# Position bias made beside the first image's tokens, parameter bounds between its scan output chunks, layer 1's inputs in other PSUM banks and its norms in later chunks

## The chip, the cores and the metric

The kernel runs on one core of a Trainium2 chip. The metric is the device time of one execution in microseconds (us); the time of a kernel is the median of its runs. The engines are named as in the profile: PE (TensorE, the matmuls), PEld (its weight loads), DVE (VectorE), ACT (ScalarE), POOL (GpSimd) and SP (SyncE, which only issues DMAs here). Each takes its own instructions in the order that was fixed when the program was built.

## The reference

Four layers, one after the other, on 4 images of 64 x 64 positions with 128 channels, all in float32. Cut to what matters here:

```python
# layer 0: selective scan in four directions k (rows, columns, and both backwards)
xc    = silu(depthwise_conv3x3(ln(x) @ in_proj_x) + conv_b)          # 256 channels
z     = ln(x) @ in_proj_z
delta = softplus(dt_w[k] @ (x_proj[k] @ xc)[:8] + dt_b[k])
h     = exp(delta * A) * h + (delta * xc) * B_t                      # along 4096 positions
y     = sum over k of (h . C_t) + Ds * xc
x     = x + (ln(y) * silu(z)) @ out_proj
x     = x + gelu(ln(x) @ fc1) @ fc2
# layer 1: attention over all 4096 positions, 16 query/key channels
f, g, v = x @ Wq, x @ Wk, x @ Wv
x     = gamma * (v^T softmax(f g^T, over n)) + x
# layer 2: 1x1 and 3x3 convolutions with hard swish
# layer 3: attention in a 7 x 7 neighbourhood, 4 heads, with a position bias rpb, then an MLP
attn  = softmax(q k^T + rpb[relative position]);  x = x + (attn v) @ proj
x     = x + gelu(ln(x) @ fc1) @ fc2
```

The kernel computes the softmaxes of layers 1 and 3 and the softplus of layer 0 without subtracting a maximum. For that it computes bounds of the exponents' sizes from the parameters and from layer 1's queries, keys and values into a tile `K.bounds`. At the end it reads one word made of them, and would do the whole network again in a general form if a bound were exceeded. With these inputs it isn't.

## The kernel before

**Phases.** An image's work has two halves. The first is *scan inputs* (`scan_inputs`): the *tokens* (`scan_tokens`: layer norm, in_proj, 3 x 3 convolution as nine diagonal matmuls L246, SiLU, in 8 chunks of 512 positions) leave `xc` in SBUF; the *steps* (`scan_steps`) make `delta` and `du = delta * xc` (L417 on POOL) and the rows B and C (`bc`) for four directions, and store all of these in DRAM. The scan itself (`selective_scan`) then goes through the directions in the order 1, 3, 0, 2, and in each through 8 chunks, 2 halves, 4 groups of states and 2 pairs: 512 *units* to an image. A unit loads its `bct` on SP, makes `dB` on POOL (L499), two `dA = exp(A * delta)` on ACT (L505, into PSUM), two recurrences on DVE (L507), and two products with C on DVE (L512) or, in 5 of 16 units for the first image and 7 of 16 for the others, one on POOL (L520). PE sums the products (L553). The last direction, 2, goes from chunk 7 to chunk 0 and stores each chunk of `y` in DRAM as it is made.

The second half is `rest`: *scan output* (`scan_output`: in 8 chunks from 7 to 0, load `y`, norm, gate, out_proj and MLP into `xT`; two chunks are under way at a time, each a generator that gives way at its `yield`s; the MLP of layer 3 of the image before runs between them), `layer1`, `layer2`, `layer3_attention`. The last image's `rest` runs after the scan's memory has been given back (`scan_over`), and its attention layers use wider tiles (`wide`).

**Order.** A planner places each instruction when the program is built. Where several are ready for an engine it takes the lowest number. Plain code is numbered from near 0 upwards. `selective_scan` has numbers from 10,000,000 (`SCAN_FIRST`), so the scan fills what the other phases leave. `make_layer2` (folded weights for layer 2, stored in DRAM) has numbers from 5,000,000. Everything of SP goes through one queue in order, ACT's own DMAs through ACT's.

**Memory.** Pools are a stack: a pool opened after another was closed lies in the same bytes, and its tiles wait until the old tiles there are released. In PSUM (8 banks) the scan has 4 (`ss_ps`: three `dA`, one `py`), and the phase beside it the other 4.

**What stands between.** `network` calls, after the first image's scan in the text, `layer0_bound`, `layer3_bound` and `make_bias`, then the scan inputs of images 1 to 3, then `rest` of each image. These first three each open pools of their own, in the 4 PSUM banks and the SBUF that the scan inputs use. `make_bias` makes a table `T` from 256 small matmuls (L1191) and 8 additions (L1194), and from it 12 tiles `bt`: a memset (L1201), three copies out of `T` by DMA (L1212) and one store to DRAM (L1213) each.

**Layer 1's inputs.** `layer1`'s PSUM pool has one buffer for each tag. `ps` is the scores' (2 banks; 4 in the last image), `pa` and `den` have a bank each. `queries` fills `f` by four rounds of two matmuls (L755) and a copy (L756), each round in the same `ps`; `norms` squares on ACT (L744), sums by matmul (L747) and takes the maximum on DVE (L748) into `K.bounds`, again through `ps`; `keys` (L762, L763) and `values` (L770, L771) too. The norms of a block of keys come right after it: for the first one ahead of the values, for three more in chunk 0 of the attention. A step of the attention makes scores (L783), exponentials (L787) and products with `v` (L831).

Of the kernel before, what the change touches and what calls it, by code (L numbers as in the profile page):

```python
# [18 lines left out]

# [404 lines left out]
def make_scan(ctx, tc, K, A):  # L424
# [5 lines left out]
    S.psum = ctx.enter_context(tc.tile_pool(name="ss_ps", bufs=1, space=PSUM))  # L430
# [148 lines left out]
def scan_output(tc, K, A, D, img, xT, last):  # L579

    nc = tc.nc
    with ExitStack() as ctx:
# [68 lines left out]
        before = None if last is None else layer3_mlp(tc, K, A, D, *last, wpool, pool, psum, together)  # L653
# [64 lines left out]
def layer1(tc, K, A, D, img, xT, wide):  # L718
# [6 lines left out]
    with ExitStack() as ctx:  # L725
# [14 lines left out]
        def norms(src, where):  # L740
            if K.general:
                return
            sq = pool.tile([128, 2, LC], F32, name="sq", tag="e", bufs=10 // NP)
            nc.scalar.activation(sq, src, AF.Square)  # L744
            ps = pair()
            for u in range(2):
                nc.tensor.matmul(ps[0:4, u, :], K.quads, sq[:, u, :], start=True, stop=True)  # L747
            nc.vector.tensor_reduce(K.bounds[0:4, img, where : where + 1], ps[0:4, :, :], AX.XY, ALU.max)  # L748

        def queries():  # L750
            for p in range(4):
                quad = span(p, 32)
                ps = pair()
                for u in range(2):
                    nc.tensor.matmul(ps[quad, u, :], Wq, xT[:, span(2 * p + u)], start=True, stop=True)  # L755
                nc.scalar.activation(f[quad], ps[quad], AF.Identity, bias=K.first[quad, :])  # L756
            norms(f, 0)

        def keys(p):
# [4 lines left out]
            norms(g[:, 2 * p : 2 * p + 2, :], 1 + p)  # L764

        def values():
            for p in range(4):
                ps = psum.tile([128, 8, 128], F32, name="ps_v", tag="ps")
                for t in range(8):
                    nc.tensor.matmul(ps[:, t, :], xT[:, span(8 * p + t, 128)], Wv, start=True, stop=True)  # L770
                nc.scalar.activation(v[:, 8 * p : 8 * p + 8, :], ps, AF.Copy, scale=gamma)  # L771
            if not K.general:
                nc.vector.tensor_reduce(
                    K.bounds[:, img, 5:6], v, AX.XY, ALU.max, apply_absolute_value=True
                )

# [45 lines left out]
        for c in range(NCH):  # L822
# [3 lines left out]
            for t in range(8):  # L826
# [26 lines left out]
                if c == 0 and t in (1, 3, 5) and not K.general:  # L853
                    keys((t + 1) // 2)
            finish(c, pa, den)
# [201 lines left out]
def layer0_bound(tc, K, A):  # L1057
# [3 lines left out]
    with tc.tile_pool(name="l0b", bufs=1) as pool, tc.tile_pool(name="l0b_p", bufs=1, space=PSUM) as psum:  # L1061
        load = loader(tc, pool, A, 0)
        w = load("in_proj", [128, DI], A["L0_conv_in_proj_w"][:, :DI])
        ln_w, ln_b = load("ln1_w", [128, 1]), load("ln1_b", [128, 1])
        conv_w, conv_b = load("conv_w", [128, ND, 9]), load("conv_b", [128, ND])
        x_proj, dt_w = load("x_proj_w", [128, ND, 2, 128]), load("dt_w", [128, 2, DI])
        squares = pool.tile([128, DI], F32, name="squares")
        nc.scalar.activation(squares, w, AF.Square, scale=ln_w)
        nc.scalar.activation(w, w, AF.Abs, scale=ln_b)
        for t in (conv_b, x_proj, dt_w):  # L1070
            nc.scalar.activation(t, t, AF.Abs)
        ps = psum.tile([128, 2, ND], F32, name="ps")
        for i, t in enumerate((squares, w)):
            for d in range(ND):
                nc.tensor.matmul(ps[:, i, d : d + 1], t[:, span(d, 128)], K.ones[:, 0:1], start=True, stop=True)
        m = pool.tile([128, ND], F32, name="m")
        nc.vector.tensor_copy(m, ps[:, 0, :])
        nc.gpsimd.tensor_tensor(m, m, bc(K.half, [128, ND]), ALU.pow)
        nc.vector.scalar_tensor_tensor(m, m, C**0.5, ps[:, 1, :], ALU.mult, ALU.add)
        taps = pool.tile([128, ND], F32, name="taps")  # L1080
        nc.vector.tensor_reduce(taps, conv_w, AX.X, ALU.add, apply_absolute_value=True)
        nc.vector.tensor_mul(m, m, taps)
        nc.vector.tensor_add(m, m, conv_b)
        pr = psum.tile([128, 2], F32, name="pr")
        for o in range(2):
            for d in range(ND):
                nc.tensor.matmul(
                    pr[:, o : o + 1], x_proj[:, d, o, :], m[:, d : d + 1], start=(d == 0), stop=(d == ND - 1)
                )
        rows = pool.tile([128, 2], F32, name="rows")  # L1090
        nc.scalar.activation(rows, pr, AF.Identity, bias=K.first2)
        pd = psum.tile([1, 2, 2, DI], F32, name="pd")
        for o in range(2):
            for b in range(2):
                at = slice(64 * b, 64 * b + 1 + R)
                nc.tensor.matmul(pd[:, b, o, :], rows[at, o : o + 1], dt_w[at, o, :], start=True, stop=True)
        most = pool.tile([1, 1], F32, name="most")
        nc.vector.tensor_reduce(most, pd, AX.XYZ, ALU.max)
        nc.vector.tensor_scalar(most, most, STEP_LIMIT, None, ALU.is_le)
        nc.vector.tensor_scalar(K.bounds[0:1, 0, 6:7], most, -1.0, 1.0, ALU.mult, ALU.add)  # L1100


def layer3_bound(tc, K, A):
# [5 lines left out]
    with tc.tile_pool(name="lb", bufs=1) as pool, tc.tile_pool(name="lb_p", bufs=1, space=PSUM) as psum:  # L1109
        load = loader(tc, pool, A, 3)  # L1110
        w = load("qkv_w", [128, 3 * C])
        b = load("bq", [1, 3, C], A["L3_conv_qkv_b"].rearrange("(o p) t -> o t p", o=1))
        ng = load("ng", [1, C], A["L3_conv_norm1_g"].rearrange("p o -> o p"))
        nb = load("nb", [1, C], A["L3_conv_norm1_b"].rearrange("p o -> o p"))
        rp = load("rp", [1, HEADS * 169], A["L3_conv_rpb"].rearrange("(o a) b -> o (a b)", o=1))
        for t in (w, b, ng, nb, rp):
            nc.scalar.activation(t, t, AF.Square)
        ps = psum.tile([1, 3 * C], F32, name="ps")
        nc.tensor.matmul(ps, K.ones[:, 0:1], w, start=True, stop=True)

        r = pool.tile([1, 2 * n + 3], F32, name="r")
        nc.vector.tensor_reduce(r[:, :n], ps.rearrange("o (h d) -> o h d", d=HD), AX.X, ALU.add)
        nc.vector.tensor_reduce(r[:, n : 2 * n], b.rearrange("o t (h d) -> o (t h) d", d=HD), AX.X, ALU.add)
        nc.vector.tensor_reduce(r[:, 2 * n : 2 * n + 1], ng, AX.X, ALU.max)
        nc.vector.tensor_reduce(r[:, 2 * n + 1 : 2 * n + 2], nb, AX.X, ALU.add)
        nc.vector.tensor_reduce(r[:, 2 * n + 2 :], rp, AX.X, ALU.max)
        nc.gpsimd.tensor_tensor(r, r, bc(K.half[0:1, :], [1, 2 * n + 3]), ALU.pow)
        a = pool.tile([1, 1], F32, name="a")
        nc.vector.scalar_tensor_tensor(
# [625 lines left out]
```

## Time and profile before

| | us |
|---|---|
| median of 3 runs | 9234.54 (9232.48 to 9246.47) |
| the profiled execution | 9231.94 |
| its span, first to last instruction | 9230.1 |
| busy: PE, DVE, POOL, ACT | 7385.0, 7119.9, 7049.3, 5664.3 |
| granted TensorE clock, mean | 0.852 |

When the phases run, from the trace (us from the span's start; the scan by its first and last L499, `rest` by its first L596 and the next one's):

| image | tokens | scan | rest |
|---|---|---|---|
| 0 | 18 to 215 | 255 to 2434 | 2338 to 4161 |
| 1 | 608 to 941 | 2434 to 4307 | 4161 to 6125 |
| 2 | 1261 to 1487 | 4307 to 6203 | 6125 to 8079 |
| 3 | 1811 to 2031 | 6203 to 8072 | 8079 to 9230 |

The table gives spans of phases that overlap: while one image is scanned, the scan inputs of all later images (during image 0) or the `rest` of the image before run beside it. A window of the profile gives busy time of each engine within it, with the number of instructions, then the granted TensorE clock, the share of the DMA engines' time and the rate of the transfers. A line of the timeline gives start, duration, engine, line, operation, output and inputs, shapes, how many instructions were merged, and in brackets how long the engine had been idle and what ended that.

### The profile page before, as it was taken

The numbers are of one execution on the slowest core, as the hardware profiler recorded it, in microseconds if no ns is written. First come the engines' busy times: TensorE is split into PE (matmuls) and PEld (weight loads), VectorE is DVE, ScalarE is ACT, GpSimd is POOL, SyncE is SP. The second block draws the span as 40 slices with busy tenths as digits, with TensorE's granted clock in tenths as the row PEclk, the third lists the DMA queues.
The fourth block names the chain that finished last, engine by engine and source line by source line (L and its number), as shares of the span: only waits on it lengthen the run. The fifth ranks groups of instructions, "written<-read, shape, count | busy, mean of one in ns | idle before, by whom it ended". The sixth has DMA issues, their size and how long they took to land. (4 is left out here: it accounts for less than half of the span.)

```text
span 9230.1 us, 99135 instructions
## 1 busy us (share of the span) xinstructions
PE 7385.0 (80%) x30116; PEld 2800.0 (30%) x30116; DVE 7119.9 (77%) x8479; ACT 5664.3 (61%) x11293; POOL 7049.3 (76%) x3064
## 2 busy tenths in 40 slices
PE   7647768697678998887689987877799888877987
PEld 3212222132322232333322232334222323343333
DVE  0698777777899988988899979988899889812433
ACT  4655666666566666666766666667666666554355
POOL 1977988979889988997799979988899889900000
PEclk9658678696789998888889988888899988889989
DMA  2766766767544545555444545565455455520020
GB/s 73 268 219 220 258 216 215 247 211 272 202 150 173 175 159 199 182 205 186 153 171 169 182 166 190 190 207 175 153 187 174 156 195 191 183 68 4 1 83 29
DMA packets 716654, 1581.74 MB, mean 171 GB/s; under 512 B 203317, under 2 KB 328396, under 8 KB 711757
## 3 DMA queue, kind: packets, MB, share of 16 engines
q1 hardware_dynamic: 585805, 1399.10, 44.3%
q10 hardware_dynamic: 130304, 176.19, 5.4%
q8 instruction: 242, 3.96, 0.2%
q14 instruction: 303, 2.48, 0.1%
HBM read 1280.47 MB, written 283.59 MB: 169 GB/s over the span
## 5 line engine op out<-in xcount | busy, mean ns | idle before, releaser
L499 POOL TENSOR_TENSOR dB<-du,bc 128x1024 f32<-128x1024 f32 x2048 | 4791.2, 2362 | 639.1 <-DMA bc<-bc_dram 170.9
L505 ACT ACTIVATE dA<-dt,w_A_log 128x512 f32<-128x512 f32 x4096 | 2777.7, 689 | 553.5 <-DVE hc L507 262.6
L507 DVE TENSOR_TENSOR_SCAN dA<-dA,state,dB 128x512 f32<-128x512 f32 x2128 | 2625.6, 1272 | 339.1 <-POOL dB L499 173.7
L520 POOL TENSOR_TENSOR hc<-hc,bc 128x1024 f32<-128x1024 f32 x832 | 1961.8, 2361 | 165.2 <-ACT state L516 92.3
L507 DVE TENSOR_TENSOR_SCAN hc<-dA,state,dB 128x512 f32<-128x512 f32 x1456 | 1802.9, 1268 | 285.8 <-ACT dA L505 118.1
L512 DVE TENSOR_TENSOR hc<-dA,bc 128x512 f32<-128x512 f32 x2432 | 1561.3, 676 | 121.6 <-PE py L553 112.2
L553 PE MATMUL py<-hc,pick 128*32 128x512 f32 x8192 | 1262.5, 696 | 277.6 <-POOL hc L520 180.0
L514 ACT COPY state<-dA 128x1 f32<-128x1 f32 x2128 | 325.4, 157 | 1295.3 <-DVE hc L512 1270.0
L831 PE MATMUL pa<-e,l_v 128*128 128x512 f32 x2048 | 1069.0, 653 | 10.9 <-ACT e L787 10.7
L783 PE MATMUL pair<-l_g,l_f 32*128 32x512 f32 x2048 | 531.4, 667 | 180.1 <-ACT e L787 134.9
L787 ACT ACTIVATE e<-pair 128x1024 f32<-128x1024 f32 (+1 forms) x448 | 507.8, 1133 | 207.0 <-PE pair L783 205.5
L831 PEld LDWEIGHTS pa<-e,l_v 128*128 128x128 f32 x2048 | 373.5, 199 | 664.3 <-issue 639.3
L553 PEld LDWEIGHTS py<-hc,pick 128*32 128x32 f32 x8192 | 216.9, 118 | 1065.5 <-issue 488.9
L507 DVE TENSOR_TENSOR_SCAN dA<-dA,dB 128x512 f32<-128x512 f32 x304 | 357.3, 1212 | 229.1 <-POOL dB L499 175.7
L409 PE MATMUL ps<-xdbl,w_dt_w 9*128 9x512 f32 x512 | 346.5, 899 | 220.5 <-ACT delta L360 142.4
L1281 PE MATMUL pair<-table,ident 128*128 128x512 f32 x768 | 417.4, 670 | 114.1 <-ACT e L1291 89.7
L246 PE MATMUL ps<-band,w_conv_diag 128*128 128x504 f32 (+3 forms) x1152 | 493.1, 586 | 3.4 <-ACT band L315 1.7
L417 POOL TENSOR_TENSOR du<-delta,xc 128x1024 f32<-128x1024 f32 x128 | 333.8, 2611 | 191.0 <-ACT delta L360 179.6
L200 PE MATMUL ps<-ident,ln_xn 128*128 128x128 f32 x512 | 129.7, 350 | 313.1 <-ACT ln_xn L197 240.9
L1291 ACT ACTIVATE e<-pair 128x1024 f32<-128x1024 f32 (+1 forms) x224 | 254.3, 1135 | 149.4 <-PE pair L1285 149.0
L218 PE MATMUL ps<-xnT,w_fc_w 128*128 128x512 f32 x512 | 281.6, 687 | 71.5 <-ACT xnT L201 29.4
L246 PEld LDWEIGHTS ps<-band,w_conv_diag 128*128 128x128 f32 x1152 | 217.3, 190 | 279.1 <-issue 257.8
(276 smaller groups left out, 8616.2 us busy)
## 6 DMA issues: line engine op xcount, KB each, us to landing
bc<-bc_dram SPq DMA_DIRECT2D x1024, 512.0 KB
dt<-delta_dram SPq DMA_DIRECT2D x512, 512.0 KB
du<-du_dram SPq DMA_DIRECT2D x512, 512.0 KB
delta_dram<-delta ACTq DMA_DIRECT2D x128, 512.0 KB
du_dram<-du SPq DMA_DIRECT2D x128, 512.0 KB
table<-biasT_dram SPq DMA_DIRECT2D x72, 512.0 KB
y_first_dram<-y_sum ACTq DMA_DIRECT2D x128, 256.0 KB
y_before<-y_first_dram SPq DMA_DIRECT2D x128, 256.0 KB
```

What stands on the lines that cost most here:

```text
L246: mm = nc.tensor.matmul(out[:, r0 - row0 : r1 - row0, c0:c1], lhsT((dy + 1) * 3 + dx + 1), src[:, r0 + dy : r1 + dy, c0 + dx : c1 + dx], s ...
L409: nc.tensor.matmul(pd[:, d, :], dt_w[rows, o, d * 128 : (d + 1) * 128], xdbl[rows, i, :], start=True, stop=True,)
L499: nc.gpsimd.tensor_mul(dB, dus[pp], mid(bct[:, 0, :], 2))
L505: nc.scalar.activation(dA, dts[pp][:, g, :], AF.Exp, scale=S.A[:, k, j, pr, g : g + 1])
L507: nc.vector.tensor_tensor_scan(hg[:, order], dA[:, order], dB[:, g, order], 0.0 if i == 0 else state[:, j, pr, g : g + 1], ALU.mult, ALU.add,)
L512: mm = nc.vector.tensor_mul(hc[:, g, :], dA, bct[:, 1, :])
L520: made.append(nc.gpsimd.tensor_mul(hc, hc, mid(bct[:, 1, :], 2)))
L553: mm = nc.tensor.matmul(py[0][32 * q : 32 * q + 32, :], S.pick, hcs[q // 2][:, q % 2, :], start=(k == 1 and j == 0), stop=(j == NJS - 1),)
L783: nc.tensor.matmul(ps[:, u, :], f[quad, t // 4, span(t % 4, 128)], g[quad, c, :], start=True, stop=True)
L787: made = nc.scalar.activation(e, ps, AF.Exp)
L831: nc.tensor.matmul(pa, v[:, 8 * q + t, :], es[q], start=(t == 0 and q == 0), stop=(t == 7 and q == 3),)
L1281: nc.tensor.matmul(ps[:, u, :], K.ident, t[:, u, :], start=True, stop=False)
```

## The change

- `make_bias` moves to the start of the program, ahead of the scan inputs of image 0 in the text, with `make_layer2`'s numbers (from 5,000,000). It and `make_layer2` take SBUF from the other end (`side="right"`), one after the other in the same bytes; the bias's PSUM pool is the 4 banks that the scan will use. `bt` has one buffer instead of two. The scan's PSUM pool is opened later, at that same end.
- `layer0_bound` and `layer3_bound` become generators that use `scan_output`'s pools and give way after each matmul group. In the first image's scan output they run between the chunks, in the place that layer 3's MLP has for later images. `layer0_bound` takes its last maximum in four parts.
- `queries` does all eight matmuls into one `ps` tile, neighbours writing to different quarters of its partitions, and one copy. `values` goes through `pa` and `den` in turn, 8 tiles of one bank instead of 4 of two.
- The norms, and the maximum over `v`, move from behind queries, keys and values to the fourth step of chunks 1 to 5.

```diff
 def network(tc, A, out):
             make_conv_diagonals(tc, K, A, D.conv_diag)
-            with tc.tile_pool(name="mk_w2", bufs=1) as pool:
-                with priority(tc, K, SCAN_FIRST // 2):
+            with priority(tc, K, SCAN_FIRST // 2):
+                make_bias(tc, K, A, D.biasT)
+                with tc.tile_pool(name="mk_w2", bufs=1, side="right") as pool:
                     make_layer2(tc, K, A, D, pool)
-                scan_inputs(tc, K, A, D, 0)
+            scan_inputs(tc, K, A, D, 0)
+            S.psum = scan_ctx.enter_context(tc.tile_pool(name="ss_ps", bufs=1, space=PSUM, side="right"))
...
                 if img == 0:
-                    layer0_bound(tc, K, A)
-                    layer3_bound(tc, K, A)
-                    make_bias(tc, K, A, D.biasT)
                     for later in range(1, B):
                         scan_inputs(tc, K, A, D, later)
 def scan_output(tc, K, A, D, img, xT, last):
-        before = None if last is None else layer3_mlp(tc, K, A, D, *last, wpool, pool, psum, together)
+        before = None
+        if last is not None:
+            before = layer3_mlp(tc, K, A, D, *last, wpool, pool, psum, together)
+        elif not K.general:
+            before = chain(layer0_bound(tc, K, A, wpool, psum), layer3_bound(tc, K, A, wpool, psum))
 def layer1(tc, K, A, D, img, xT, wide):
         def queries():
-            for p in range(4):
-                quad = span(p, 32)
-                ps = pair()
-                for u in range(2):
-                    nc.tensor.matmul(ps[quad, u, :], Wq, xT[:, span(2 * p + u)], start=True, stop=True)
-                nc.scalar.activation(f[quad], ps[quad], AF.Identity, bias=K.first[quad, :])
-            norms(f, 0)
+            ps = pair()
+            for u in range(2):
+                for p in range(4):
+                    nc.tensor.matmul(ps[span(p, 32), u, :], Wq, xT[:, span(2 * p + u)], start=True, stop=True)
+            nc.scalar.activation(f, ps, AF.Identity, bias=K.first)
         def keys(p):
...
             nc.scalar.copy(g[:, 2 * p : 2 * p + 2, :], ps)
-            norms(g[:, 2 * p : 2 * p + 2, :], 1 + p)
         def values():
-            for p in range(4):
-                ps = psum.tile([128, 8, 128], F32, name="ps_v", tag="ps")
-                for t in range(8):
-                    nc.tensor.matmul(ps[:, t, :], xT[:, span(8 * p + t, 128)], Wv, start=True, stop=True)
-                nc.scalar.activation(v[:, 8 * p : 8 * p + 8, :], ps, AF.Copy, scale=gamma)
-            if not K.general:
+            for n in range(8):
+                ps = psum.tile([128, 4, 128], F32, name="ps_v", tag=("pa", "den")[n % 2])
+                for q in range(4):
+                    nc.tensor.matmul(ps[:, q, :], xT[:, span(8 * q + n, 128)], Wv, start=True, stop=True)
+                nc.scalar.activation(v[:, n::8, :], ps, AF.Copy, scale=gamma)
+        def bounds(n):
+            if n == 0:
+                norms(f, 0)
                 nc.vector.tensor_reduce(
                     K.bounds[:, img, 5:6], v, AX.XY, ALU.max, apply_absolute_value=True
                 )
+            else:
+                norms(g[:, 2 * n - 2 : 2 * n, :], n)
...
                 if c == 0 and t in (1, 3, 5) and not K.general:
                     keys((t + 1) // 2)
+                if c > 0 and t == 3 and c <= 5 and not K.general:
+                    bounds(c - 1)
 def make_bias(tc, K, A, out):
-        pool = ctx.enter_context(tc.tile_pool(name="bias", bufs=1))
-        psum = ctx.enter_context(tc.tile_pool(name="bias_p", bufs=4, space=PSUM))
+        pool = ctx.enter_context(tc.tile_pool(name="bias", bufs=1, side="right"))
+        psum = ctx.enter_context(tc.tile_pool(name="bias_p", bufs=4, space=PSUM, side="right"))
...
-                bt = pool.tile([128, HEADS, RC, W], F32, name="bt", bufs=2)
+                bt = pool.tile([128, HEADS, RC, W], F32, name="bt")
```

## The prediction

> **What bounds the kernel now.** I read the busy time by stage first, since the page's shares average over stages with different limits. The cuts are events of the timeline: the scan's products L499 run from 255 us, and those of its four images end at 2434, 4307, 6203 and 8072; the later layers of each image (its first L596) begin at 2338, 4161, 6125 and 8079.
>
> ```profile
> core 0: us, PE busy (x) PEld busy (x) DVE busy (x) ACT busy (x) POOL busy (x), PEclk, DMA share, GB/s
> 520.00:766.00 246.00, 98.88 (x566) 34.30 (x566) 233.15 (x288) 123.58 (x304) 178.62 (x82) 0.58 0.75 238
> 766.00:950.00 184.00, 166.66 (x496) 66.22 (x497) 139.32 (x163) 121.88 (x253) 134.69 (x59) 0.95 0.55 192
> 1260.00:1490.00 230.00, 201.75 (x606) 78.88 (x604) 170.47 (x216) 153.81 (x339) 160.43 (x69) 0.92 0.54 178
> 1770.00:1886.00 116.00, 77.63 (x242) 27.98 (x243) 100.47 (x147) 79.05 (x189) 102.33 (x45) 0.76 0.61 217
> 4161.00:4600.00 439.00, 321.06 (x1300) 159.46 (x1300) 367.90 (x521) 311.98 (x692) 345.52 (x149) 0.84 0.51 172
> 4600.00:5346.00 746.00, 657.62 (x2664) 201.39 (x2664) 683.92 (x727) 484.84 (x919) 726.66 (x315) 0.93 0.50 173
> 8072.00:8385.00 313.00, 240.75 (x892) 137.34 (x890) 55.91 (x204) 161.65 (x338) 2.07 (x1) 0.87 0.17 53
> ...
> ```
>
> POOL is the scan's limit: beside layer 1 (4600 to 5346) it is busy 97%. A unit of the scan (one L499; 512 to an image) costs POOL 2.36 us, plus 2.36 for the share that L520 does there (5 of 16 units in the first image, 7 of 16 later): 3.10 and 3.39 us. That turns POOL time into units. But the scan isn't the only chain. The later layers of images 0, 1 and 2 follow one another without a gap (2338, 4161, 6125, 8079), each taking some 1955 us against the scan's 1870 to 1900, and they fall behind: the second image's begin 146 us before its scan ends, the third's 78 us, the last's 7 us after. So **the chain of later layers sets the end**: the last image's scan output runs alone (8072 to 8385, POOL idle), though seven of its eight inputs were ready.
>
> The second view is the timeline of SyncE and ScalarE around 760 us.
>
> ```profile
> 748.60 1.67 SPq L490 DMA_DIRECT2D bc<-bc_dram  x1
> 750.39 3.79 SPq L1213 DMA_DIRECT2D biasT_dram<-bt  x2
> ...
> 766.61 1.28 ACT L342 ACT_TABLE_LOAD   x1
> 767.90 1.27 ACT L342 ACTIVATE xc<-ps,w_conv_b 128x512 f32<-128x512 f32 x2
> ```
>
> The second image's first xc is written 12 us after the last bias store is issued, although its tokens had begun at 608. xc lies where the bias pool lay, and waits for it. Steps of the first image end near 520; then come the bounds (to 553) and the bias (to 766). The second image's tokens end at 941, the third's take 226 us (1261 to 1487). Without the two they would end near 520 + 226 = 746: **195 us** earlier, and with them all scan inputs and the 2338.
>
> The third view is layer 1's start in the last image.
>
> ```profile
> 8385.05 1.90 PE L755 MATMUL pair<-xT,w_Wq 128*32 128x512 f32 x4 [0.84 <-DVE x L1570]
> 8387.13 1.10 ACT L756 ACTIVATE l_f<-pair,first 32x1024 f32<-32x1024 f32 x1 [3.63 <-PE pair L755]
> 8388.29 1.90 PE L755 MATMUL pair<-xT,w_Wq 128*32 128x512 f32 x4 [1.33 <-ACT l_f L756]
> ...
> 8398.68 3.56 PE L747 MATMUL pair<-sq,quads 128*4 128x512 f32 x4 [2.28 <-ACT sq L744]
> 8402.33 1.21 DVE L748 TENSOR_REDUCE bounds<-pair 4x1 f32<-4x1024 f32 x1 [17.33 <-PE pair L747]
> 8403.60 1.98 PE L762 MATMUL pair<-xT,w_Wk 128*128 128x512 f32 x4 [1.36 <-DVE bounds L748]
> ```
>
> One buffer, `ps`, holds everything, so PE, ScalarE and DVE take turns. From the first query to the first `pa` (8431.47) it takes 46 us.
>
> **The change, part by part.** The sum is made against the profiled execution (9231.9 us, span 9230.1). The median is 2.6 above it.
>
> A. Bias and bounds leave the first scan. From 520 to 766 POOL did 178.6 / 3.10 = 58 units. At the rate with least beside it (1770 to 1886: 102.3 / 3.10 = 33 units, 3.51 us each) these take 202 us, so 44 were lost. Part of that is tokens work that comes anyway: tokens cost the scan 230 - 51.7 x 3.51 = 48 us (1260 to 1490) and only 31 of it shows after 766. 44 - 17 = 27: **-27** (0 to -44). The bounds' small instructions come back beside the first image's scan output, which then waits for the scan; cover gone, they cost their old 33 us (520 to 553), in the high end.
>
> B. Bias beside the first tokens (0 to 255). Its 256 matmuls L1191 take 14.9 us of a PE that is busy 199 of 255; half: **+8**. DVE is busy 14 us of the 255 and hides the 12 memsets (21.2 us). The 36 copies and 12 stores join SyncE's queue, in order, ahead of x loads; `bt` has one buffer now, so a store waiting for its copies holds the loads behind it. Two x buffers cover one chunk, some 25 us, against 163 / 12 = 14 us a group in the busy queue of before. make_layer2 follows the bias in the same bytes, and its L873 (20.8 us on POOL) can land on the scan's start: high end 14.9 + 20.8 = 36. Low end 0.
>
> C. The later layers start earlier. Scan inputs done 195 us sooner, the first image's scan output can follow the scan's last direction (1886 to 2434), chunk by chunk. It then ends with that scan plus one chunk: 65 us (the first chunk took 2342 to 2406). Before, layer 1 began 204 us after the scan's end, when POOL had done 178.4 / 3.39 = 53 units (2434 to 2641); now 17. The lead is 36 units, at layer 1's 3.48 us (746 us for 214 units) **125 us**. What is late next is the scan itself, so 195 isn't kept.
>
> D. Layer 1's inputs. Queries: 16 instructions with neighbours in other column quarters. L553 is of that kind: 8 in 1.06 us (timeline), so 2.1 us and one copy of 1.10 in place of four rounds of 3.1. Keys 1.98 and 1.01. Values: 8 x 1.03 us, in two other banks, while ScalarE copies. First `pa` after some 14 us, not 46: -32. The three norms in chunk 0 held the scores 3.2 us each (8445.6 to 8448.8): -10. Later, each of five costs PE 1.88 and, at worst, reduce 1.3 and an exposed wait on `e` of 2.0; 3.6 taken: +18. So **-24** in the last image (-6 to -33), and -23 in each other one.
>
> The Trainium skill, TensorE: Matmul & The Clock Gate, section Part 3: Packing small matmuls, says that a weight load overlaps matmuls in flight only when its row group differs, which speaks against the queries' new order, as all four share the 128 rows. By it 16 loads at the measured 0.11 us of L755 would be exposed, an estimate of 1.8 us. L553's row, same shape, shows 8 loads and matmuls in 1.06 us, so I leave it out.
>
> E. What the lead is worth. 125 + 3 x 23 = 194 us before the last image. One chunk of scan output beside the scan takes 439 / 8 = 55 us, so 3.5 chunks move under the scan. Alone each takes 306 / 8 = 38. Under it, each costs the scan (439 - 101.8 x 3.48) / 8 = 10.6. Net -27.5 each: **-96** (1 chunk -27, 6.5 chunks -179).
>
> Sum: -27 + 8 - 24 - 96 = -139, so 9093 for the execution and **9095 us** for the median. Its own range, from the terms' ends, is 8980 (-44, 0, -33, -179) to 9210 (0, 36, -6, -27 give 9237, all four at once being rare).
>
> **Rivals.** *The lead goes nowhere* (0.17). POOL's 97% beside layer 1 says that each engine's fixed order ties the later layers to the scan's units; shorter preludes then only leave less room for units. Against it: the lag does grow, 146, 78, -7. Then A, B and D alone: 9234.5 - 43 = 9191. *The chain catches up* (0.25): all eight chunks but the last follow the last scan, 7 x -27.5 = -193, sum -236: 8999. For it: the layers of image 1 already start 146 us ahead; against it, 3.5 chunks are what the rows give. *Slower* (0.10): the first image's scan output chases the scan. PE and ScalarE take their queues in order; a matmul L613 placed ahead of its y (stored by ScalarE, loaded by SyncE) stops the scan's L553 behind it, so hc buffers fill and POOL stops. Against it: next to the second image's scan output units take 3.9 us, without such holes, though there most y were ready. Eight chunks must lose over 139 / 8 = 17 us each to decide; at 25 us: 9295. *It doesn't do what it says* (0.05): bias and make_layer2 outlast the tokens and hold the scan's start. At the bias's old 163 us, of which 100 come late, 9195.
>
> **Numbers.** Forecast 0.43. What a measurement can tell from no change is about 0.2%, 18 us. Faster 0.84: all but the slower case and the tails of the first and last rival. Same 0.06, slower 0.10. Range 8975 to 9220: down past the catching up, up to the lead that goes nowhere with B's high end.
>
> **What would show it.** Right: the second image's tokens right after 520, the last image's L596 near 7890 and well before the last L499, the first `pa` 14 us after the first query, L748 only in chunks 1 to 5, L1191 before 100 us. Wrong: the first L499 after 275; PE idle on y loads near 2300; the last image's L596 still at the scan's end, which is the first rival.

## The result, and the profile after

| | before | after | predicted |
|---|---|---|---|
| median, us | 9240.51 (4 runs, 9232.48 to 9246.61) | 9158.21 (4 runs, 9149.27 to 9166.0) | 9095 (8975 to 9220) |
| ratio | | 0.9911, 95% interval 0.9894 to 0.9928 | |
| the profiled execution and its span | 9231.94, 9230.1 | 9166.0, 9164.3 | 9093 |

The change makes the kernel 0.9% faster. That lies in the range, but the gain of the profiled execution is 66 us where the sum said 139. The differences between runs below are between medians, those between phases between single profiled executions.

Phases by the same cuts as before (us from the span's start). "Query" is the first matmul of layer 1's queries.

| | before | after |
|---|---|---|
| first image's tokens | 18 to 216 | 21 to 247 |
| first L499 | 255 | 295 |
| second image's tokens | 608 to 942 | 571 to 776 |
| last scan inputs done | 2331 | 2161 |
| ends of the four scans | 2434, 4307, 6203, 8072 | 2465, 4355, 6257, 8158 |
| last image: scan output starts, query, first `pa` | 8079, 8385, 8431 | 7950, 8318, 8333 |
| last image: attention chunks | 343 long | 366 long |

The busy time by stage of the kernel after, to be laid beside the stages shown of before: tokens of the second image, scan output and layer 1 of the second image, and the last image's scan output up to the last scan's end (8158) and behind it.

```profile
core 0: us, PE busy (x) PEld busy (x) DVE busy (x) ACT busy (x) POOL busy (x), PEclk, DMA share, GB/s
571.00:776.00 205.00, 183.06 (x562) 74.16 (x564) 154.54 (x196) 145.00 (x340) 144.50 (x62) 0.96 0.52 175
4065.00:4506.00 441.00, 325.36 (x1304) 163.06 (x1308) 366.46 (x521) 314.66 (x698) 345.02 (x149) 0.83 0.54 177
4506.00:5230.00 724.00, 642.42 (x2640) 198.42 (x2634) 668.27 (x711) 473.20 (x914) 708.70 (x306) 0.94 0.49 171
7950.00:8158.00 208.00, 161.90 (x626) 84.97 (x630) 167.59 (x244) 143.50 (x316) 156.38 (x68) 0.83 0.53 176
8158.00:8318.00 160.00, 124.53 (x474) 68.24 (x466) 33.30 (x106) 87.16 (x178) 2.36 (x1) 0.88 0.09 29
```

Layer 1 is as full as before (POOL 708.70 of 724, 98%). The last two rows are the gain: of the last image's scan output, which before ran 306 us alone (8079 to 8385) with POOL idle, 208 us now run beside the last 47 units of the scan and 160 us remain behind it.

The timeline of SyncE's queue after the first loads: start, duration, what it issues.

```profile
52.65 4.70 SPq L1226 DMA_DIRECT2D bt<-T  x4
57.47 1.77 SPq L305 DMA_DIRECT2D x<-in_x  x1
...
89.85 0.33 SPq L1227 DMA_DIRECT2D biasT_dram<-bt  x1
90.22 0.43 SPq L305 DMA_DIRECT2D x<-in_x  x1
...
122.47 2.16 SPq L1226 DMA_DIRECT2D bt<-T  x3
124.67 1.43 SPq L305 DMA_DIRECT2D x<-in_x  x1
```

The loads of the token chunks 5, 6 and 7 stand between copies and stores of the bias. Before, they were issued at 51, 76 and 103. The waits from 0 to 255 say why (us in total, how often, the longest):

```profile
POOL w_diag L889 <- DMA biasT_dram<-bt: 208.3, 1, 208.3
DVE bt L1215 <- DMA biasT_dram<-bt: 109.9, 11, 13.2
...
PEld ps L312 <- ACT xnT L202: 41.0, 7, 15.8
...
ACT xnT L202 <- DMA bt<-T: 19.3, 3, 12.5
```

Eleven of the twelve memsets of `bt` wait for the store before them, the copies in SyncE's queue wait for the memset, and PE waits for tokens (41.0 us, where it was 25.5 before). ScalarE has a wait of its own, the last row: its stores of `sz` and `xc` stand in its queue until a bias copy has landed, and its work on the next tokens stands behind them. The transfers of both queues take turns on the same semaphores; in the trace the store issued at 206.70 waits for the one that the copy issued at 201.77 raises.

The first row is make_layer2, which waits for the bias's bytes and lets its long power (now L881) run from 232 to 253 on POOL. It does not hold the first du on POOL, but by way of SyncE's queue. These lines are from the timelines of SyncE, PE and POOL, the first one before, the others after:

```profile
215.91 0.34 SPq L165 DMA_DIRECT2D w_x_proj_w<-in_L_conv_x_proj_w  x1
...
254.38 0.33 SPq L915 DMA_DIRECT2D w_cv_dram<-w_cv  x1
...
255.88 0.33 SPq L166 DMA_DIRECT2D w_x_proj_w<-in_L_conv_x_proj_w  x1
...
259.03 7.19 PE L396 MATMUL ps<-xc,w_x_proj_w 128*128 128x512 f32 x8 [13.14 <-DMA w_x_proj_w<-in_L_conv_x_proj_w]
...
272.10 5.66 POOL L418 TENSOR_TENSOR du<-delta,xc 128x1024 f32<-128x1024 f32 x2 [17.76 <-ACT delta L361]
```

The weights of the steps are issued behind stores of make_layer2 that come right after the power, so the steps start 12 us after the tokens' end (4 before), and POOL stands idle for 17.76 us ahead of the first du.

The start of layer 1 in the last image, from the timeline:

```profile
8318.15 1.92 PE L757 MATMUL pair<-xT,w_Wq 128*32 128x512 f32 x16 [0.83 <-DVE x L1584]
...
8320.27 1.11 ACT L758 ACTIVATE l_f<-pair,first 128x1024 f32<-128x1024 f32 x1 [3.67 <-PE pair L757]
...
8332.84 3.70 PE L837 MATMUL pa<-e,l_v 128*128 128x512 f32 x8
```

One round of queries and one copy, and the first `pa` comes 14.7 us after the first query, where it took 46.4.

### The profile page after: what moved, and what is told of

Its sections match the earlier page's. It is cut to its first block, busy times and chain, and to the rows that moved or that the text cites. A ratio compares the mean times of both kernels' runs of the same rounds, so it can differ in the third digit from the quotient of the medians.

```text
span 9164.3 us, 99142 instructions
## 1 busy us (share of the span) xinstructions
PE 7366.3 (80%) x30116; PEld 2795.3 (31%) x30116; DVE 7110.9 (78%) x8483; ACT 5639.9 (62%) x11293; POOL 7049.8 (77%) x3064
## 5 line engine op out<-in xcount | busy, mean ns | idle before, releaser
L499 POOL TENSOR_TENSOR dB<-du,bc 128x1024 f32<-128x1024 f32 x2048 | 4799.9, 2369 | 679.1 <-DMA bc<-bc_dram 217.6
L553 PE MATMUL py<-hc,pick 128*32 128x512 f32 x8192 | 1239.9, 688 | 249.0 <-POOL hc L520 195.8
L837 PE MATMUL pa<-e,l_v 128*128 128x512 f32 x2048 | 1081.0, 660 | 17.9 <-ACT e L793 17.7
L789 PE MATMUL pair<-l_g,l_f 32*128 32x512 f32 x2048 | 539.8, 678 | 196.7 <-ACT e L793 148.1
L837 PEld LDWEIGHTS pa<-e,l_v 128*128 128x128 f32 x2048 | 381.5, 203 | 687.9 <-issue 638.2
L789 PEld LDWEIGHTS pair<-l_g,l_f 32*128 32x128 f32 x2048 | 141.1, 191 | 549.8 <-ACT e L793 277.1
```

Of the source, the lines that this page charges most:

```text
L499: nc.gpsimd.tensor_mul(dB, dus[pp], mid(bct[:, 0, :], 2))
L553: mm = nc.tensor.matmul(py[0][32 * q : 32 * q + 32, :], S.pick, hcs[q // 2][:, q % 2, :], start=(k == 1 and j == 0), stop=(j == NJS - 1),)
L789: nc.tensor.matmul(ps[:, u, :], f[quad, t // 4, span(t % 4, 128)], g[quad, c, :], start=True, stop=True)
L837: nc.tensor.matmul(pa, v[:, 8 * q + t, :], es[q], start=(t == 0 and q == 0), stop=(t == 7 and q == 3),)
```

## The experiments

### Which part gives what

**Layer 1's edits alone**, everything else as before:

```diff
 def layer1(tc, K, A, D, img, xT, wide):
-            for p in range(4):
+            ps = pair()
+            for u in range(2):
...
+                if c > 0 and t == 3 and c <= 5 and not K.general:
+                    bounds(c - 1)
```

> The kernel before with layer 1's edits alone (queries in one tile, values in two other banks, norms in chunks 1 to 5). Theory (the chain of later layers sets the end, and its lead is worth 27 us for each chunk of scan output that moves under the last scan): the last image's layer 1 is about 9 us shorter from first query to last pa (46 + 343 before, 15 + 366 with the whole change), the three other images gain some 18 us each, 54 us of lead, one chunk, -27: about -36 us, ratio 0.996. Rival (the bias move gives nothing, all of the -82 us comes from layer 1): ratio 0.991.

Measured 9207.69, ratio 0.9963 (0.995 to 0.9975). The last scan output starts at unit 2023 of 2048; the preludes (query to first `pa`) are 17, 19, 25 and 15 us.

**The change without layer 1's edits**:

```diff
 def layer1(tc, K, A, D, img, xT, wide):
-            ps = pair()
-            for u in range(2):
+            for p in range(4):
...
-                if c > 0 and t == 3 and c <= 5 and not K.general:
-                    bounds(c - 1)
```

> The whole change without layer 1's edits (bias beside the first tokens, bounds between the scan output chunks). Theory: the scan starts 40 us late as with the whole change; the later layers reach the last image some 150 us before the scan's end, 2.8 chunks at -27: -77 + 40 = about -37 us, ratio 0.996, the last image's first L596 near 8000. Rival (the bias move gives nothing): no change or up to 40 us slower, ratio 1.000 to 1.004.

Measured 9212.26, ratio 0.9966 (0.9954 to 0.9979). The first L499 is at 295 and the last scan output starts at 8022.

**The bias alone moved**; the bounds stay between the first image's steps and the second's tokens:

```diff
                 if img == 0:
+                    layer0_bound(tc, K, A)
+                    layer3_bound(tc, K, A)
                     for later in range(1, B):
```

> The bias alone is moved; both bounds stay behind the first image's scan inputs, layer 1 as before. Theory (the first image's scan output waits for the scan's y anyway, so 33 us of bounds ahead of the scan inputs cost nothing): within 10 us of the run with bias and bounds moved. Rival (every us of the scan inputs counts): 33 us of lead less, about half a chunk, 15 us slower than that run.

Measured 9206.22, ratio 0.9958 (0.9942 to 0.9975): no worse than with the bounds moved too. The first image's query comes at 2531, against 2535 with the bounds moved. So the two halves of the change (layer 1's edits; bias and bounds) give 0.37% and 0.34%, together somewhat less than its 0.89%, though not outside the intervals, and moving the bounds gave nothing that shows.

### What the norms cost where they are now

**No norms at all**, nor the maximum over `v`, so that this kernel leaves out those bounds:

```diff
-                if c > 0 and t == 3 and c <= 5 and not K.general:
-                    bounds(c - 1)
```

> The whole change, but the norms of queries and keys and the maximum over v are left out (their columns of the bounds stay 0). Theory (each late norm holds the scores some 7 us in the last image, where a chunk with a norm takes 47 us and one without took 40): the last image's layer 1 is 34 us shorter, the others some 20 us each, 60 us of lead, one chunk, -27: about -60 us against the whole change, ratio 0.985 against before. Rival (beside the scan POOL sets the pace and a norm costs nothing there): -34 us, ratio 0.987, pa phases of the first three images as long as with the norms.

Measured 9028.21, ratio 0.9766 (0.975 to 0.9782): 130 us under the changed kernel, far more than either theory. The last image's chunks, from 366 to 330, show the price best, since nothing runs beside them. The timeline of PE around the second norm of the changed kernel's last image:

```profile
8442.49 3.70 PE L837 MATMUL pa<-e,l_v 128*128 128x512 f32 x8
...
8454.25 1.88 PE L750 MATMUL pair<-sq,quads 128*4 128x512 f32 x4
8457.44 1.14 PE L789 MATMUL pair<-l_g,l_f 32*128 32x512 f32 x8 [1.30 <-DVE bounds L751]
8460.58 1.32 PE L789 MATMUL pair<-l_g,l_f 32*128 32x512 f32 x8 [2.00 <-ACT e L793]
8461.83 5.17 PE L837 MATMUL pa<-e,l_v 128*128 128x512 f32 x8
```

The norm's matmuls take 1.88 us. Then PE waits 1.30 us, until DVE has reduced the one scores buffer that the norm went through, and 2.00 us more, since the next scores need that buffer again after its exponential. Then the same eight L837 take 5.17 us, not 3.70. Windows of 1 us of the same stretch show why (the clock is the third number from the end):

```profile
8459.00:8460.00 1.00, 0.00 (x0) 0.00 (x0) 0.00 (x0) 1.00 (x1) 0.00 (x0) 1.00 0.00 0
...
8462.00:8463.00 1.00, 1.00 (x2) 0.48 (x3) 0.85 (x1) 1.00 (x1) 0.00 (x0) 0.50 0.00 0
8463.00:8464.00 1.00, 1.00 (x3) 0.48 (x2) 0.09 (x1) 0.88 (x1) 0.00 (x0) 0.50 0.00 0
...
8465.00:8466.00 1.00, 1.00 (x4) 0.40 (x3) 1.00 (x1) 0.00 (x0) 0.00 (x0) 1.00 0.00 0
```

The granted clock falls to half after the two pauses, and comes back some 3 to 4 us later. The same follows each of the five norms: against 1.14 for eight L789 and 3.70 for eight L837, the matmuls behind them lose 1.62, 1.65, 1.70, 2.82 and 2.65 us, 2.09 on the mean. So a late norm costs 1.88 + 1.30 + 2.00 + 2.09 = 7.3 us, and five 36, which is the 366 - 330.

**Norms at a chunk's end**, through `den`'s bank, with squares in a buffer of their own:

```diff
-            sq = pool.tile([128, 2, LC], F32, name="sq", tag="e", bufs=10 // NP)
+            sq = pool.tile([128, 2, LC], F32, name="sq")
-            ps = pair()
...
+                ps = psum.tile([128, LC], F32, name="ps_n", tag="den")
...
+            if 1 <= c <= 5 and not K.general:
+                bounds(c - 1)
```

> The whole change, but the norms run after a chunk's finish, through the den bank, one half at a time, with a square buffer of their own, in place of the scores' buffer ps and a buffer e. Theory (a late norm costs by holding ps and e, so that scores, exponentials and products wait in turn): most of the 130 us that leaving them out gained come back, last image's pa phase 330 to 342 us, the first three 655 to 670, total 9035 to 9065 us, ratio 0.978 to 0.981. Rival (the cost is the norms' own work on PE, ScalarE and DVE): little comes back, pa phase near 360, ratio 0.988 or more.

Measured 9149.32, ratio 0.9902 (0.9886 to 0.9919). The chunks are shorter, 661, 684, 678 and 340 us (changed kernel: 699, 689, 709, 366), as the theory has it for the first and last image. But the last scan ends at 8213, 55 us later than in the changed kernel, and the total hardly moves. Both theories miss: what layer 1 gained, the scan beside it lost.

**All keys and norms ahead of chunk 0**, a norm in two halves through `pa` and `den`:

```diff
+                ps = psum.tile([128, LC], F32, name="ps_n", tag=("pa", "den")[u])
+                nc.tensor.matmul(ps[0:4, :], K.quads, sq[:, u, :], start=True, stop=True)
+                nc.vector.tensor_reduce(tops[:, u : u + 1], ps[0:4, :], AX.X, ALU.max)
...
+            for p in range(1, 4):
+                keys(p)
+            for n in range(5):
+                bounds(n)
```

> The changed kernel with keys 1 to 3 and all norms put back ahead of the first attention chunk; a norm now takes one bank at a time, of the two that attention is not yet using, so none waits for the projections' pairs; nothing of them is left inside the chunks. Theory (the norms are dear where they stand: their instructions and waits in the middle of the chunks lengthen each of them, 47 us a chunk against 40): the chunk phases fall from 699/689/709/366 us to about 655/660/665/332, the time from the last image's first query's start to the first chunk grows from 15 to about 30, the last image's layer 1 with its prelude is some 18 us shorter, the total 9060 to 9090, ratio 0.981 to 0.984. Rival (it is the norms' own work, which has only been moved): the prelude grows by as much as the chunks lose, 25 to 35 us in each image, and the total stays at 9140 to 9170, ratio 0.989 to 0.992.

Measured 9121.07, ratio 0.9868 (0.985 to 0.9886), between the two theories. In the last image there was more to gain than the theory's 18 us: prelude 29 and chunks 317, together 346, against 15 + 366 = 381 in the changed kernel and 15 + 330 = 345 without any norm. There the place was the whole cost, though keys 1 to 3 left chunk 0 as well. The windows of the last image's chunks, first of the changed kernel, then with the norms first:

```profile
8333.00:8699.00 366.00, 340.59 (x1176) 132.03 (x1180) 158.13 (x104) 132.30 (x85) 0.00 (x0) 0.96 0.00 0
```

```profile
8346.00:8664.00 318.00, 315.06 (x1160) 123.56 (x1156) 150.03 (x100) 126.01 (x78) 0.00 (x0) 1.00 0.00 1
```

PE now rests 3 us of 318, not 25 of 366, and the mean clock is 1.00, not 0.96. Beside the scan it is different. Layer 1 from query to last `pa` takes 695, 690 and 684 us (changed kernel: 718, 713, 728; no norms: 669, 678, 677), but the last scan ends at 8190, against 8158 and 8112. The last scan output starts 26 us earlier and its query at the same 8317. So of the 130 us, 37 come from the place. The other 93 remain with norms and keys in the preludes, most of them as a later scan end (78 us). Whether that is the norms' own work, or the preludes of the first three images (57 to 61 us long, 18 to 22 without norms), no run here separates.

### What delays the start of the scan

**The memsets of `bt` on POOL**:

```diff
-                nc.vector.memset(bt, FAR)
+                nc.gpsimd.memset(bt, FAR)
```

> The whole change, but the 12 memsets of bt run on POOL, which is idle before the scan, in place of DVE. Theory (with one bt buffer a memset waits for the store before it, and the first tokens' layer norm statistics wait behind it on DVE): tokens of the first image end near 225 instead of 247, first L499 near 272 instead of 295, total about -20 us against the whole change. Rival (what delays the tokens is their x loads, queued on SyncE behind copies and stores): first L499 stays within 5 us of 295, total as with the whole change.

Measured 9173.31, ratio 0.9924 (0.9907 to 0.9941). Tokens end at 252, the first L499 is at 292, and the late x loads still go at 59, 92 and 126. So DVE's queue is not what holds them; SyncE's is tried below.

**make_layer2 ahead of the bias**, in bytes of its own:

```diff
-                make_bias(tc, K, A, D.biasT)
                 with tc.tile_pool(name="mk_w2", bufs=1, side="right") as pool:
                     make_layer2(tc, K, A, D, pool)
+                    make_bias(tc, K, A, D.biasT)
```

> The whole change, but make_layer2 stands ahead of make_bias and in bytes of its own, so its powers on POOL (20.8 us) are done before 70 us and not at 232 to 253. Theory (the scan's start is late by two things, 31 us in the tokens and 9 us from the powers just ahead of the first du): first L499 near 286, total -9 us against the whole change. Rival (the powers hide behind the first steps' matmuls): first L499 stays at 295. A bias that starts later could also push its copies into the scan, and the first L499 past 295.

Measured 9296.76, ratio 1.0071 (1.0054 to 1.0088). Something else happened than was tried: with these bytes more, the tokens' weights lie where the bias lies and wait for it ("ACT xnT L202 <- DMA w_ln_b" for 168 us). The tokens run from 198 to 395, the scan starts 140 us late, at 435, and the total is 139 us higher. A start so late is paid in full.

**Four buffers for the token tiles**, so that x loads are issued earlier:

```diff
-                xt = pool.tile([128, 4, 128], F32, name="x")
+                xt = pool.tile([128, 4, 128], F32, name="x", bufs=4)
```

> The changed kernel with four buffers in place of two for the token tiles, so that SyncE issues the loads of chunks 6 and 7 without a wait, ahead of the bias's copies. Theory (what makes the first tokens 31 us later is SyncE's queue, where those loads stand behind copies that wait for the bias): the loads issue before 60 us, the tokens end near 225 (247), the first L499 starts near 272 (295), the total falls by about 20 us to 9135 to 9142, ratio 0.9885. Rival (the tokens are late because DVE and POOL do the bias's work first): the first L499 stays within 5 us of 295 and the total within 6 us of 9158.

Measured 9135.94, ratio 0.9882 (0.9864 to 0.99, which overlaps the changed kernel's interval a little). The last x loads are issued at 20, 31 and 55, and the first image's tokens end at 231, nearly as expected. Yet the first L499 is only at 290, not 272. The timelines of POOL and ScalarE have the reason:

```profile
232.44 20.82 POOL L881 TENSOR_TENSOR w_last<-w_last,mhalf 128x128 f32<-128x128 f32 x1 [0.18 <-POOL w_norms L880]
...
241.69 16.38 ACTq L405 DMA_DIRECT2D bc_dram<-xdbl  x3
...
263.90 0.22 POOL L880 TENSOR_SCALAR w_norms<-w_raw 128x1 f32<-128x1 f32 x1 [9.59 <-DMA w_raw<-in_L_conv_bn_cat]
...
264.74 5.66 POOL L418 TENSOR_TENSOR du<-delta,xc 128x1024 f32<-128x1024 f32 x2
```

The power now holds the first du in two ways. ScalarE's stores of `bc` take 16.38 us to issue (2.46 before), since they wait for transfers that SyncE issues only after the power, so the first delta is there at 260. Then POOL's last norm of make_layer2, whose load also comes after the power, holds the du to 264.7. The total is as forecast by another way: each later image's tokens also start sooner after the steps before them (18, 22 and 25 us, not 30, 31 and 34), and the last scan inputs end 32 us earlier.

**The power replaced** by a multiplication, in the changed kernel, which then leaves out the scale of that norm:

```diff
-        nc.gpsimd.tensor_tensor(out[:, 0, :], out[:, 0, :], K.mhalf[:rows, :width], ALU.pow)
+        op = ALU.pow if width == 1 else ALU.mult
+        nc.gpsimd.tensor_tensor(out[:, 0, :], out[:, 0, :], K.mhalf[:rows, :width], op)
```

> The changed kernel with one instruction of make_layer2 replaced: the power over the last layer 2 norm's 128 columns (20.8 us on POOL between the first image's tokens and its steps) becomes a multiplication, so that norm's scale is not computed. Theory (the power holds the first du): the steps start some 16 us after the tokens' end in place of 25, the first L499 starts at 286 (295), the total is 9 us lower, 9146 to 9152, ratio 0.990. Rival (the steps' own weights and matmuls are what ends last there): the first L499 stays at 293 to 297 and the total within 5 us of 9158.

Measured 9161.71, ratio 0.9909 (0.9889 to 0.9928). One of the four executions took 13630.58 us, for a reason that no run here shows, and is in that median but not in the ratio; the other three took 9149.54 to 9167.15, with a median of 9156.27. The first du comes 18 us after the tokens' end, not 25, nearly as the theory says, but not because POOL was held: the weights of the steps are issued at 251.55, at the tokens' end, and the first L396 starts 4 us after it. The first L499 is at 294, since here the tokens end at 252. In the five kernels that share the changed kernel's start (it, and those without layer 1's edits, without norms, with norms at a chunk's end and with norms first) the tokens end at 247 to 250 and the first L499 lies at 295 to 299, so 2 us are no more than that spread, and nothing shows in the total.

**Norms first and four buffers**:

```diff
+                xt = pool.tile([128, 4, 128], F32, name="x", bufs=4)
...
+            for n in range(5):
+                bounds(n)
```

> Both edits together. If each does what its theory says they add, since one shifts the start of every stage and the other shortens layer 1: some 20 us and some 80 us under the changed kernel, 9040 to 9070, ratio 0.979 to 0.982. If neither does, 9140 to 9170.

Measured 9089.31, ratio 0.9837 (0.9819 to 0.9854). It is 69 us under the changed kernel, where the two gave 37 and 22 by themselves. They at least add up, short of the forecast 9040 to 9070, which took the norms' place for 80.

**The same, and the power after the first image's last du**:

```diff
+            scan_inputs(tc, K, A, D, 0)
+            with tc.tile_pool(name="mk_w2", bufs=1, side="right") as pool:
+                make_layer2(tc, K, A, D, pool)
...
+        if width > 1:
+            after(tc, made, K.du)
```

> The kernel with the norms first and four token buffers, and make_layer2 behind the first image's inputs, with its long power on POOL after the last du of that image, so it runs beside the scan. Theory (the power holds the first du there by 18 us, since du starts 34 us after the tokens' end against 16 in the kernel before, and POOL has room beside the scan): the first L499 starts near 271 (289), the total is 12 to 18 us under that kernel's 9089, 9070 to 9078, ratio 0.982. Rival (the scan waits for POOL for as long as the power takes, wherever it is put): the first L499 starts as early, but the scan's first image takes 15 to 20 us longer and the total stays at 9084 to 9094.

Measured 9069.85, ratio 0.9816 (0.98 to 0.9833): the fastest version here, some 88 us under the change as given. The two last intervals overlap a little, so the 19 us of this step are likely rather than certain. The timeline of POOL:

```profile
252.50 5.66 POOL L418 TENSOR_TENSOR du<-delta,xc 128x1024 f32<-128x1024 f32 x2 [17.41 <-ACT delta L361]
...
275.53 11.57 POOL L499 TENSOR_TENSOR dB<-du,bc 128x1024 f32<-128x1024 f32 x5 [3.38 <-DMA du<-du_dram]
```

The first L499 comes at 276, not 289. As the rival said, the scan pays for the power anyway: it runs at 531 to 552 between two units, and the first scan ends at 2455 against 2458. The gain goes with another difference again: the last scan inputs end 32 us earlier, and with them the later layers start.

## Why the prediction was right or wrong

The mechanism was right: freed of bias and bounds, the scan inputs end 170 us earlier (195 predicted), the later layers no longer end behind the scan, and the last scan output slips under the last scan. The size was not: the time lies in the range because the range's high end allowed for a B and a D as dear as these, and the sum itself forecast twice the gain. Its terms in the order of the chain that sets the end, each measured between the two profiled executions:

| term | predicted | measured |
|---|---|---|
| A and B: end of the first scan | -27 + 8 = -19 | +31 (2434 to 2465) |
| scans of images 1 and 2 | 0 | +23 (1873 to 1890, 1896 to 1902) |
| E: last scan, longer by the scan output beside it | 3.5 x 10.6 = +37 | +32 (1868 to 1901) |
| E: last scan output behind the scan's end | 3.5 x -38 = -133 | -153 (313 to 160) |
| D: last image's prelude | -32 | -32 (46.4 to 14.7) |
| D: last image's chunks | -10 + 18 = +8 | +23 (343 to 366) |
| from the last chunk to the end | 0 | +10 |
| sum | -139 | -66 |

The rows are not independent: a scan that ends later (the second row) leaves more of the last scan output beside it (the fourth).

**A and B failed**, and they are 50 of the 73 us. B's step said that the bias beside the first tokens costs half of its PE time, +8, with the queue and the power at the high end (36). The first L499 is 40 us later, and one "after 275" was the prediction's own first sign of being wrong. "Two x buffers cover one chunk, some 25 us" was the wrong weight: the loads did fall behind, and tokens end 31 us later. Another 8 us are the weights of the steps, issued behind the power. The runs show holds in series. Taking the loads ahead moved the first L499 by 5 us, taking the power out by 2, and loads ahead with make_layer2 behind the tokens (and the norms first, which do not touch that stretch) by 20. In the other 20 us the tokens still end 17 us later than before. There ScalarE waits 6.1 and 6.2 us for bias copies, and 15.2 us ahead of its last `xc`, where it waited 10.8 for PE before: about as much, but no run took these waits out. A's 27 us came as 9 (the first scan took 2179, now 2170 us); where the rest went was not tried. That the bounds cost nothing beside the first scan output agrees with the two runs that differ in them.

**C and E held**, measured against the scan. Layer 1 of the first image begins 72 us after its scan's end (65 predicted, 204 before). The lead at the last image is 47 units, 208 us (56 units and 194 us predicted). In absolute time it is less: the last image's L596 comes at 7950, not near 7890, and the scan itself ends 86 us later than before. Half of a lead reaches the end, as E's 27.5 of 55 us says: the last scan output starts 129 us earlier, and its layer 1 67 us earlier. E's 10.6 us for each chunk beside the scan are not shown by themselves: without norms, 275 us of scan output lie beside a last scan that takes 1885 us, 17 longer than before.

**D's prelude was exact**, the late norms were mis-sized. "Later, each of five costs PE 1.88 and, at worst, reduce 1.3 and an exposed wait on `e` of 2.0; 3.6 taken": both waits come in full, and the halved clock behind them adds 2.1, so 7.3 each. The trace of before could have told, since its norms in chunk 0 have both waits, and the clock is at 0.50 there from 8454 to 8456:

```profile
8445.60 1.88 PE L747 MATMUL pair<-sq,quads 128*4 128x512 f32 x4
8448.79 1.14 PE L783 MATMUL pair<-l_g,l_f 32*128 32x512 f32 x8 [1.30 <-DVE bounds L748]
8451.92 1.14 PE L783 MATMUL pair<-l_g,l_f 32*128 32x512 f32 x8 [2.00 <-ACT e L787]
```

In the first three images layer 1 is 14, 22 and 17 us shorter from query to last `pa`, where 23 were taken. That a norm stays dear beside the scan in each of the places tried was not seen at all. The 23 us of the two middle scans stay open; without norms the second of the four scans is 31 us shorter than in the changed kernel, the third 1.

On the queries, the Trainium skill (TensorE: Matmul & The Clock Gate, Part 3: Packing small matmuls) would have added an estimated 1.8 us, since the weights share their rows. The 16 loads and matmuls took 1.92 us in all, by the row above, where the prediction had 2.1; no load shows as idle time of PE.

**Rivals.** The lead that goes nowhere did not happen: 47 units of it were used. Nor did the catching up: the last scan output is 160 us behind the scan, not one chunk. PE blocked by the first image's `y` did not either, as units from that scan output's first L596 to the query take 3.94 us, against 4.06 before. The bias holding the scan's start happened in small, 40 us, and in full where make_layer2 was put first (9297 us).

## What to carry to other kernels

A piece of work moved into a stretch "with room" is priced by what shares its queue: list the loads behind it, when each is needed, and what waits for the bytes that it gives back. Holds in series hide each other, so a part that gains nothing alone may gain with the next one removed. And an instruction on one engine can hold another through a third's queue: look for what stands behind it there. A small reduction that goes through the one buffer of a tight matmul loop costs both of its turns in that buffer, several times its own instruction.

## What was not expected of the hardware

Two pauses of PE of 1.3 and 2.0 us, with 1.14 us of matmuls between them, were followed by a fall of the granted clock from 1.00 to 0.50 for 3 us and more, after each of five norms. Even one pause can be enough: chunk 0 of the changed kernel's last image has three single pauses of 2.00 us, up to 8348.19, 8362.83 and 8375.82, and the clock is at 0.50 from 8349 to 8352 and from 8377 to 8379, but at 1.00 from 8362 to 8367. The Trainium skill (TensorE: Matmul & The Clock Gate, Part 1: The HAM clock gate) puts the fall after an idle window of some 3.4 us. No pause of PE in these chunks was that long.

Norms were thought to be nearly free for the scan, and here they are not: their own work in the last image is 10.5 us on DVE (five reductions of 1.2 us and one of 4.4), 5.3 on ACT and 9.4 on PE. Yet without them the last scan ended 78 us earlier than with all of them in the preludes. Three images' worth of that DVE time would be 32 us, if all of it held the scan. What makes the 78 was not settled.
